# Four hand-placed reorderings in a tuned float32 graph layer: second x tile in front of the taps, first product weights of group two by hand, combined weights late, last transposes behind the last product

## The chip, the cores and the metric

The kernel runs on one core of one Trainium2 chip. The metric is the device time of one execution in microseconds (us). Most executions agree within 0.3%; each kernel was run several times beside the kernel before on the same chip, and all runs quoted here are of the same (fast) state. One execution of each kernel was also profiled. A profiled run is one sample. Engines: PE is TensorE, DVE is VectorE, ACT is ScalarE, POOL is GpSimd, SP is SyncE, which here only issues transfers.

## The reference

x is 32 x 512 x 256, adj is 32 x 512 x 512, all float32. Cut to what matters:

```python
h = jnp.maximum(_layernorm(x), 0.0)
xc = h.transpose(0, 2, 1)
c = relu(bn1(conv1(xc)))              # 1x1 convolution, 256 -> 256
c = bn2(conv2(c))                     # 17 taps
x_conv = relu(c + xc)
s = h @ w_se.T + b_se                 # three features a node
A = exp(-dist(s)) * adj
x_nmp = A @ relu(h @ w_msg.T + b_msg)
# GRU: r, z, n from [x_conv, x_nmp] and h
out = x + (1 - z) * n + z * h
```

## The kernel before

The 17-tap convolution is done by windows in the frequency domain. The 32 samples ("tiles" below) are worked in two groups of 16, one after the other:

1. `first_part`: layer norm, transposes, first convolution, transform of each tile. In group one the taps of the second convolution are transformed in between ("tap products", `weights_to_freq`). In group two POOL combines the GRU weights for a Strassen-like scheme in between (`combine_weights`, 12 steps for three weights).
2. `nodes`: messages, affinities, aggregation for 16 tiles, with the products of the frequency units ("product") in between. A product's weights are two tiles of 256 KB in DRAM, loaded in turn, and their sum, made on POOL.

After both groups comes the gate part: 16 pairs of tiles, inverse transform and 84 + 42 large matmuls a pair. The parts inside `manual_schedule` run in the order of the text on each engine; the others are put in order by a scheduler, which may move an instruction far forward if its operands and its buffer allow it. On each engine the order is fixed when the kernel runs.

The parts that the change touches:

```python
def statistics(b):            # DVE: bn_stats x4, bn_aggr x4, + eps; then the power on POOL
    ...
    nc.gpsimd.tensor_tensor(rstd, rstd, minus_half[:, :NC], op=ALU.pow)

def product(pw, g, u, xf):
    load_unit(pw, g, u)                                        # 2 x 256 KB, tag wt, 3 buffers
    ...
        nc.gpsimd.tensor_tensor(both[:, 0], re, im, op=ALU.add)
        nc.gpsimd.tensor_tensor(both[:, 1], im, re, op=ALU.subtract)
        wsum = pw.tile([P, DC, D], FP, tag="wsum", bufs=2)
        nc.gpsimd.tensor_tensor(wsum, wr, wi, op=ALU.add)
    ...

def first_part(g, xf, between):
    b0, b1 = g * GB, (g + 1) * GB
    for b in range(b0, b0 + 3):
        if b not in X:
            load_x(b)
    statistics(b0)
    normalise(b0)
    if g == 0:
        one, two = between(b0)                                 # two steps of tap products
        for step in one: step()
        transpose_h(b0)
        for step in two: step()
    statistics(b0 + 1)
    normalise(b0 + 1)
    if g > 0:
        transpose_h(b0)
    for b in range(b0, b1):
        if b + 3 < b1: load_x(b + 3, nc.gpsimd)
        if b == b0:    conv1(b)
        if b + 2 < b1: statistics(b + 2)
        if b + 1 < b1: transpose_h(b + 1)
        if b + 2 < b1: normalise(b + 2)
        ...                                                    # conv1(b), between(b), windows_to_freq(b - 1)

# gate part
load_pair(0, nc.gpsimd)          # operands of pair 0, 4.1 MB, on POOL's queue
load_combined(sw, 0, 2)          # combined weights, 1.2 MB, POOL's queue
load_combined(sw, 2, 7)          # 2.9 MB
inverse(0)
for t, keep in ((HP[0], True), (NP[0], False), (CP[0], False)):
    sums(t, keep)                # four subtractions each on POOL
...
def then(i, j):                  # last pair: after each result of the last gate
    blend(p, i, j)
    if i != j:
        finish(p, j)             # 8 transposes, 2 adds, 2 stores of 256 KB
```

## Time and profile before

| | before |
|---|---|
| time, median (lowest to highest) | 1963.05 us (1961.53 to 1965.42, 4 runs) |
| profiled span | 1962.5 us |
| PE busy | 1903.5 us, 97% |
| PE idle: 0-32, 484-612, 905-940, 1883-1963 us | 14.0, 14.6, 15.3, 12.9 us |
| PE idle in the main gate stretch, 940-1883 us | 0.0 us |

PE is the bound nearly everywhere. The idle time of any other engine costs nothing unless PE ends up waiting for it, so the table to read is the one by stage, and then PE's own list of waits. The lines are in the prediction below.

### The profile page before, as it was taken

How to read it: one execution, taken by the hardware profiler on the slowest of the kernel's cores; microseconds unless marked ns; L12 is line 12 of the kernel's file. 1: busy time of each engine (PE TensorE's matmuls, PEld its weight loads, DVE VectorE, ACT ScalarE, POOL GpSimd, SP SyncE). 2: the span in 40 equal slices, each digit the busy share in tenths (PEclk: the TensorE clock that was granted, in tenths of full speed). 3: DMA queues.
4: the chain of work that ended last, by engine and by line, in shares of the span. 5: the costliest groups of instructions: out<-in, count | busy, mean ns of one | idle time of the engine just before them, and what ended most of it. 6: DMA issues, size and time to landing. Idle time of an engine off the chain costs nothing.

```text
span 1962.5 us, 21327 instructions
## 1 busy us (share of the span) xinstructions
PE 1903.5 (97%) x7328; PEld 1176.7 (60%) x7328; DVE 1129.6 (58%) x2197; ACT 545.5 (28%) x930; POOL 559.2 (28%) x554
## 2 busy tenths in 40 slices
PE   7999999999889999996999999999999999999997
PEld 4777677776778776763555554555455554555453
DVE  6776666655875666563255355544555355544555
ACT  2555333332234332332122221222122221222121
POOL 3231333433331443433312322133212322133210
PEclk9999999999899999998999999999999999999999
DMA  7998888776566787878421444134421444134410
GB/s 194 297 279 232 246 238 240 221 226 207 182 204 167 222 262 226 255 210 249 126 66 61 126 126 117 37 98 126 126 71 56 126 127 115 43 94 127 126 43 22
DMA packets 243259, 309.89 MB, mean 158 GB/s; under 512 B 14807, under 2 KB 194551, under 8 KB 243151
## 3 DMA queue, kind: packets, MB, share of 16 engines
q1 hardware_dynamic: 223679, 250.93, 43.9%
q0 software_dynamic: 7248, 25.73, 4.8%
q10 hardware_dynamic: 12224, 31.86, 4.7%
q8 instruction: 59, 0.97, 0.2%
q14 instruction: 49, 0.40, 0.1%
HBM read 201.57 MB, written 106.89 MB: 157 GB/s over the span
## 4 chain that ended last, share of the span: by engine, by line
PE 93%; DVE 2%; DMA 2%; issue 1%; SPq 1%; POOL 0%; ACT 0%; DVEq 0%; POOLq 0%
PE pg L497 29%; PE pn L497 14%; PE pn L399 11%; PE py L317 10%; PE pm L350 6%; PE pc L486 6%; PE pc L269 5%; PE px L284 3%; PE pw L213 2%; PE pd L385 2%; PE phT L256 1%; PE po L623 1%; DMA adj<-in_adj_dram 1%; DMA wt<-wd 1%; PE psl L371 1%
## 5 line engine op out<-in xcount | busy, mean ns | idle before, releaser
L399 PE MATMUL pn<-A,msg 128*128 128x512 f32 x512 | 229.5, 602 | 14.2 <-DVE A L391 14.2
L497 PE MATMUL pg<-hp,sw 128*128 128x512 f32 x448 | 229.4, 594 | 1.7 <-DVE u L529 1.7
L497 PE MATMUL pg<-np,sw 128*128 128x512 f32 x448 | 229.7, 594 | 0.0
L497 PE MATMUL pg<-cp,sw 128*128 128x512 f32 x448 | 229.2, 593 | 0.0
L475 POOL TENSOR_TENSOR hp<-hp 128x512 f32<-128x512 f32 x64 | 80.5, 1269 | 455.4 <-DMA hp<-hd 325.3
L399 PEld LDWEIGHTS pn<-A,msg 128*128 128x128 f32 x512 | 98.5, 193 | 127.9 <-issue 125.3
L512 ACT ACTIVATE rz<-rz,brz 128x512 f32<-128x512 f32 x96 | 69.3, 722 | 305.3 <-DVE rz L516 305.3
L475 POOL TENSOR_TENSOR cp<-cp 128x512 f32<-128x512 f32 x64 | 80.4, 1267 | 249.3 <-ACT cp L491 248.1
L390 DVE STREAM_TRANSPOSE at<-adj 128x512 f32<-128x512 f32 x128 | 135.9, 1095 | 26.0 <-DMA adj<-in_adj_dram 23.2
L317 PE MATMUL py<-wt,both 128*128 128x256 f32 x624 | 150.4, 384 | 0.0
L497 PEld LDWEIGHTS pg<-cp,sw 128*128 128x128 f32 x448 | 85.4, 191 | 107.7 <-issue 107.7
L497 PEld LDWEIGHTS pg<-np,sw 128*128 128x128 f32 x448 | 85.4, 191 | 107.4 <-issue 107.4
L309 POOL TENSOR_TENSOR both<-xf 128x256 f32<-128x256 f32 x78 | 59.9, 767 | 311.8 <-PE py L317 274.8
L317 PEld LDWEIGHTS py<-wt,both 128*128 128x128 f32 x624 | 114.2, 190 | 44.0 <-issue 26.5
L497 PEld LDWEIGHTS pg<-hp,sw 128*128 128x128 f32 x448 | 82.6, 190 | 93.8 <-issue 88.5
L312 POOL TENSOR_TENSOR wsum<-wt 128x512 f32<-128x512 f32 x78 | 106.3, 1363 | 87.3 <-DMA wt<-wd 72.6
L350 PE MATMUL pm<-wmsg,hT 128*128 128x259 f32 x512 | 125.6, 398 | 0.0
L269 PE MATMUL pc<-w,hT 128*128 128x256 f32 x512 | 122.9, 395 | 0.3 <-DVE hT L257 0.3
L350 PEld LDWEIGHTS pm<-wmsg,hT 128*128 128x128 f32 x512 | 122.3, 327 | 0.7
L486 PEld LDWEIGHTS pc<-back,yt 120*128 120x128 f32 x1024 | 116.9, 192 | 7.7 <-issue 7.7
L486 PE MATMUL pc<-back,yt 120*128 120x80 f32 (+1 forms) x1024 | 116.2, 274 | 0.0
L497 PE MATMUL pn<-hp,sw 128*128 128x512 f32 x224 | 115.1, 595 | 0.0
(112 smaller groups left out, 2854.0 us busy)
## 6 DMA issues: line engine op xcount, KB each, us to landing
wt<-wd SPq DMA_DIRECT2D x160, 256.0 KB, 5.3
adj<-in_adj_dram SPq DMA_DIRECT2D x128, 256.0 KB, 5.3
yd<-y ACTq DMA_DIRECT2D x80, 384.0 KB, 5.3
yt<-yd SPq DMA_DIRECT2D x60, 480.0 KB, 8.5
wd<-wst SPq DMA_DIRECT2D x64, 320.0 KB, 5.2
x<-in_x_dram SPq DMA_DIRECT2D x38, 512.0 KB, 5.3
hd<-hT SPq DMA_DIRECT2D x32, 512.0 KB, 4.7
nd<-nmp SPq DMA_DIRECT2D x32, 512.0 KB, 3.2
```

Source lines behind the costliest of these rows:

```text
L269: nc.tensor.matmul(p[:, j, :], HT[b][:, ic, c * P : (c + 1) * P], w1[:, ic, :], start=(ic == 0), stop=(ic == DC - 1))
L284: nc.tensor.matmul(p[:, j * 2 * L : (j + 1) * 2 * L], H1[b][:, c0 + j, ic * P : (ic + 1) * P], fwd, start=True, stop=True)
L309: nc.gpsimd.tensor_tensor(both[:, 0], re, im, op=ALU.add)
L312: nc.gpsimd.tensor_tensor(wsum, wr, wi, op=ALU.add)
L317: nc.tensor.matmul(dst, v[:, ic, :], w[:, ic, :], start=(ic == 0), stop=(ic == DC - 1))
L350: nc.tensor.matmul(p[:, : D + NS], chunk(HT[b][:, ic, :], c), wmsg[:, ic, :], start=(ic == 0), stop=(ic == DC - 1))
L390: nc.vector.transpose(at.rearrange("p (j k) -> p j k", k=32), ADJ[b].rearrange("p j (q c) -> p c j q", c=NC)[:, mc])
L399: nc.tensor.matmul(p, MSG[b][:, mc, dc * P : (dc + 1) * P], A[b][:, mc, :], start=(mc == 0), stop=(mc == NC - 1))
L475: nc.gpsimd.tensor_tensor(t[:, dst, :], t[:, a, :], t[:, b, :], op=sub)
L486: nc.tensor.matmul(bk[:, t0:t1], YT[p][j * W + w][:, oc * P : (oc + 1) * P], back[:, u0 : u0 + t1 - t0], start=(w == 0), stop=(w == W - 1) ...
L497: nc.tensor.matmul(bk, sw[:, k, q, o, :], terms[k][q], start=(first and i == 0), stop=(i == len(ks) - 1), skip_group_check=True)
L512: nc.scalar.activation(rz[:, g, j, :], src, AF.Sigmoid, bias=brz[:, g : g + 1], scale=1.0)
```

## The change

It has four parts, called A to D here, one for each stretch in which PE stands idle: (A) the second x tile is loaded ahead of the taps, its statistics come ahead of the first transposes, and the first tap products come behind the first convolution; (B) loads and sums of the first product weights of group two are placed by hand in the last three tiles of group two's first part; (C) most of the combined weights are loaded behind POOL's subtractions on pair 0; (D) the last output's transposes move behind the last product.

```diff
@@ B: the weight sum becomes a function of its own
+    def sum_unit(pw, g, u):
+        t = WSUM[g, u] = pw.tile([P, DC, D], FP, tag="wsum", name=f"wsum_{g}_{u}", bufs=2)
+        nc.gpsimd.tensor_tensor(t, WT[g, u][:, 0], WT[g, u][:, 1], op=ALU.add)
+
     def product(pw, g, u, xf):
-        load_unit(pw, g, u)
+        if (g, u) not in WT:
+            load_unit(pw, g, u)
+        if u > 0 and (g, u) not in WSUM:
+            sum_unit(pw, g, u)
 ...
-            wsum = pw.tile([P, DC, D], FP, tag="wsum", name=f"wsum_{g}_{u}", bufs=2)
-            nc.gpsimd.tensor_tensor(wsum, wr, wi, op=ALU.add)
+            wsum = WSUM.pop((g, u))
@@ D: finish() takes chunks, and which half of the channels to leave for last
-    def finish(p, j):
+    def finish(p, j, chunks=((0, 1), (2, 3)), wait_for=None):
 ...
@@ A: first_part
         statistics(b0)
         normalise(b0)
+        statistics(b0 + 1)
         if g == 0:
-            one, two = between(b0)
-            for step in one:
-                step()
             transpose_h(b0)
-            for step in two:
-                step()
-        statistics(b0 + 1)
         normalise(b0 + 1)
 ...
             if b == b0:
                 conv1(b)
+                if g == 0:
+                    for steps in between(0):
+                        for step in steps:
+                            step()
 ...
+            load_x(1)
             load_taps(gen, 0, nc.sync)
@@ B: group two's first part
                 def between(b):
-                    return combine[b - 2 : b - 1] if b > 1 else [], []
+                    if b == GB - 3:
+                        for u in range(3):
+                            load_unit(pools["pw"], 1, u)
+                    two = [partial(sum_unit, pools["pw"], 1, b - GB + 3)] if b > GB - 3 else []
+                    return combine[b - 2 : b - 1] if b > 1 else [], two
@@ C
         load_combined(sw, 0, 2)
+        sums(HP[0], True)
+        sums(NP[0], False)
         load_combined(sw, 2, 7)
         inverse(0)
-        for t, keep in ((HP[0], True), (NP[0], False), (CP[0], False)):
-            sums(t, keep)
+        sums(CP[0], False)
@@ D
                 def then(i, j):
+                    if (i, j) == (0, 1):
+                        finish(p, 0, [(0, 1)])
                     blend(p, i, j)
-                    if i != j:
-                        finish(p, j)
+                    if (i, j) == (0, 1):
+                        finish(p, 0, [(2, 3)])
+                        finish(p, 1, wait_for=0)
```

## The prediction

> **What bounds the kernel now.** The page gives TensorE (PE) 1903.5 us of a 1962.5 us span, 97%, and the chain of waits that ended last runs over PE for 93% of the span. So the change can only win where PE is idle (1962.5 - 1903.5 = 59 us) or runs at a lowered clock just after being idle. The first view I read after the page is therefore the table by stage (columns: stretch, its length, busy us and instructions of PE, of weight loads, of VectorE (DVE), ScalarE (ACT), GpSimd (POOL), then PE's granted clock, DMA share, GB/s):
>
> ```profile
> 0.00:32.00 32.00, 18.05 (x68) 11.88 (x69) 21.95 (x80) 5.12 (x8) 10.57 (x20) 0.93 0.88 202
> ...
> 484.00:612.00 128.00, 113.45 (x649) 102.81 (x648) 91.17 (x248) 41.68 (x97) 37.41 (x40) 0.93 0.54 186
> ...
> 905.00:940.00 35.00, 19.70 (x44) 8.24 (x44) 8.46 (x12) 3.36 (x6) 11.06 (x10) 0.71 0.72 229
> 940.00:1883.00 943.00, 943.00 (x3122) 493.44 (x3121) 474.08 (x697) 206.69 (x302) 231.27 (x184) 1.00 0.33 97
> 1883.00:1963.00 80.00, 67.06 (x175) 30.49 (x173) 48.32 (x72) 12.85 (x19) 0.00 (x0) 0.96 0.12 40
> ```
>
> PE's idle time sits in four places: 14.0 us at the start, 14.6 around the second group's first part, 15.3 where the gate part takes over, 12.9 in the tail: 56.7 of 59 us. The main gate stretch has none. The four edits aim at exactly these four places. Who ends the waits is in PE's list of waits (us in total, times, longest):
>
> ```profile
> PE pn L399 <- DVE A L391: 14.2, 1, 14.2
> PE row L157 <- DVE diag L156: 10.0, 1, 10.0
> PE phT L256 <- DVE x L245: 8.9, 1, 8.9
> PE phT L256 <- issue: 8.1, 2, 4.2
> PE po L623 <- DVE nt L612: 6.5, 3, 3.1
> ```
>
> The 10.0 us is the first arrival of data and stays. The two 4 us waits are one at 24.4 us (start) and one at 576.6 us; the second hangs on a weight-combination step of POOL that waits for its load, which the change doesn't touch. The chain in order of time (start, us, what) explains the 8.9 us:
>
> ```profile
> 487.97 9.25 DMA wt<-wd
> ...
> 497.39 0.03 POOL wsum L312
> 497.42 1.19 issue
> 498.61 1.04 POOL rstd L239
> 499.65 0.03 issue
> 499.67 0.42 DVE x L245
> ```
>
> A product-weight load of group two was hoisted by the scheduler in front of group two's first tiles; its sum on POOL waits for it, and the small power on POOL that normalisation needs stands behind it. By the timeline, DVE had that power's input ready at 492.71 + 0.17 = 492.88. Last, the transfers by queue (packets, MB, share), first 906 to 912 us, then 922 to 928 us:
>
> ```profile
> q0 software_dynamic: 437, 1.80, 91.2%
> q1 hardware_dynamic: 413, 0.21, 14.0%
> ```
> ```profile
> q1 hardware_dynamic: 1219, 1.05, 68.2%
> q0 software_dynamic: 19, 0.07, 5.2%
> ```
>
> q0 is POOL's queue (operands of pair 0, then the combined weights), q1 is SyncE's with the last adjacency tile. While both are active they move equal numbers of packets, but q0's are 1.80 MB/437 = 4.1 KB and q1's 0.5 KB. The last adjacency piece, issued at 912.12, landed only at 927.36, after q0 had run dry at 922, and PE stood from 916.04 to 930.20.
>
> **What the Trainium skill says.** "DMA: Bandwidth & Descriptors", section "Queues, rings and completion order": each DMA engine alternates between queues at packet granularity. The trace agrees: 437 to 413 packets at 906 to 912 us, 327 to 325 at 912 to 918. "TensorE: Matmul & The Clock Gate", Part 1 (the clock gate): PE drops to half clock after an idle window of about 3.4 us and needs about as much activity to recover. The trace agrees: 16 matmuls of the first convolution take 3.46 us in a steady run, 5.53 us after the 4.2 us gap at 576.6, while after the 3.11 us gap of the tail six gate matmuls took 2.59 us, full speed. Same page, "Architectural detail": DVE, ACT and POOL are strict first-in first-out. The trace agrees: the power ready at 492.88 waited behind the sum until 498.61.
>
> **Part A, second x tile ahead of the taps, tap products after the first convolution.** Today the second tile's statistics start at 19.07 and a chain of DVE and POOL steps leads to the third tile's normalise (27.79), transposes (28.31) and the second convolution (30.64), after which PE runs gapless. With x_1 issued at about 1.2, statistics(1) can run at about 12, behind normalise(0), and conv1(0) starts near 16 instead of 18.25, since one step of tap products (2.01 us) no longer precedes the transposes and another no longer the convolution. It takes 4.84 us as now and ends near 21. But the two tap steps now follow it (2 x 1.03 us at full clock) and statistics(2) stands on DVE behind their evictions: 21 + 2.1 + 0.7 = 23.8, against 24.70 today. From there the chain is as before. So this edit moves the wait rather than removing it: gain 0.9 us (estimate, between -1.5 and 2.5; the upper end if PE stays warm).
>
> **Part B, first product weights of group two placed by hand.** The loads go to tile 13 of the first part, the sums to tiles 14 and 15, where POOL has no normalisation left to serve. The power then runs at 492.9, normalise at about 494.1, transposes at 494.5 instead of 500.14: 5.6 us. The gap shrinks from 8.9 to 3.3 us, so PE may stay warm: the transposes took 2.37 against 0.87, the convolution 4.87 against 3.46, so up to 2.9 us more. I count 1 of these: 6.6 us (5 to 8.5). The six loads of 256 KB at tile 13 come when no x load is outstanding, and PE is busy through the next hand-over (291.89 of 293 us from 612 on).
>
> **Part C, combined weights 2 to 7 loaded behind the sums.** POOL issued all six loads by 908.5. Now only three (1.2 MB with the pair's 4.1 MB) come first, then eight subtractions, then the other 2.9 MB. q0's bytes without those 2.9 MB were through at about 913 (summing its queue figures stretch by stretch). POOL: sums(HP) from 903.7, 5.2 us; sums(NP) when its operand has landed, 896.43 + 13.3 = 909.7 for the first half and perhaps 911 for the second, then 5.2 us: 916.5. So q0 is empty from about 913 to 918 (issue plus start-up). In that hole q1 has to finish some 1700 packets (three and one adjacency pieces of 512 packets, a store of 128, less 468 done); at 1219 packets in 0.682 x 6 = 4.1 us of full use that is 5.7 us. The last adjacency piece thus lands at 918 to 920, by a narrow margin; what is left over competes again with packets of 7.7 KB. I take 919.5. From landing to PE's restart was 930.20 - 927.36 = 2.84 us, so PE restarts at 922.3 rather than 930.2: 7.9 us, range 1 (race lost) to 13. The half clock after the gap (9.65 us for the last aggregation, 6.87 warm) stays. The late weights land by about 929 and are first needed at 922.3 + 9.65 + 7.1 (inverse) + 10.3 (24 gate products) = 949: no new wait.
>
> **Part D, the last transposes behind the last product.** Today the eight transposes of the first output stand ahead of the last six gate matmuls (2.59 us) and wait 3.11 us for a blend. Then follow add, sigmoid, multiply, add, transposes, and this row ends DVE's work:
>
> ```profile
> 1957.79 1.29 DVE L625 TENSOR_TENSOR x<-x,po 128x512 f32<-128x512 f32 x2 [0.75 <-PE po L623]
> ```
>
> Without them the last matmuls run 1947.2 to 1949.8, under the blend that ends at 1950.50. Then on DVE: add 0.7 (1951.2), ACT sigmoid 0.73 beside one output add (1951.95), multiply and add 1.4 (1953.4), three output adds of 0.65: 1955.35 against 1957.79 + 1.29 = 1959.08, 3.7 us. Three stores of 256 KB now follow each other closely, which I let cost 0.3: 3.4 us (2.5 to 4).
>
> **Sum.** 0.9 + 6.6 + 7.9 + 3.4 = 18.8 us. 1964.0 - 18.8 = 1945.2 us.
>
> **Rivals.** (1) C loses its race: the three late loads start before the adjacency is through, which then lands at 925 to 928 as today. For it: the hole is five microseconds and the need is more than five. Against it: most of the queue's packets would be through. Time 1952. (2) C wins everything, PE passing from one aggregation to the next with a gap under 3 us and staying warm: another 5 + 2.8 us, 1937 to 1938. Against it: q1 is starved by the pair's operands up to 913 anyway. (3) A gets worse: tap products between first convolution and second transposes stall statistics(2), taps or x_2 land later; it costs 2, total 1948. (4) B's removed hoist makes another instruction stand in front on POOL or SyncE (the weight buffers are three and taken, so I see none): B falls to 0, total 1952.
>
> **Range and chances.** The sum of the good ends (2.5 + 8.5 + 13 + 4) gives 1936, of the bad ends (-1.5 + 5 + 1 + 2.5) 1957. Range for 8 in 10: 1935 to 1955. Two per cent are 39 us, two thirds of all of PE's idle time, of which 10 us at the start can't go; so faster by over 2% has 0.03. Slower by over 2% would need a new wait at every tile: 0.01.
>
> **What would show it.** A: statistics(2) still at about 24 and the second convolution at 29 to 30. B: no weight sum on POOL between the last product and group two's second convolution, the 8.9 us wait at 3 to 4. C: the 14.2 us wait for A at 5 to 7, SyncE's queue moving about 1 MB between 913 and 918 while POOL's is empty. D: no wait of transposes ahead of the last six matmuls, and 3 to 4 us less from the end of the product before to the end. The main stretch (943 us) must not change. Wrong would be a new wait at tile 13 to 15 or in the first gate product.

## The result, and the profile after

The changed kernel takes 1941.89 us (median; 1940.58 to 1944.33, 4 runs), against 1963.05 us: ratio 0.9893, 95% interval 0.9875 to 0.9910. Ratios here are the mean time of one kernel's fast runs over the mean of the other's fast runs of the same rounds, so not quite the ratio of the medians. The prediction was 1945.2 us (1935 to 1955).

The table by stage of the changed kernel (same columns as in the prediction) has its main gate stretch and its tail some 23 us earlier:

```profile
0.00:32.00 32.00, 18.47 (x89) 13.16 (x90) 24.96 (x87) 5.96 (x10) 11.39 (x21) 0.95 0.89 226
...
484.00:612.00 128.00, 119.04 (x685) 107.97 (x685) 95.29 (x271) 45.89 (x104) 40.74 (x44) 0.97 0.61 201
...
905.00:940.00 35.00, 27.13 (x107) 16.07 (x108) 12.73 (x17) 6.54 (x9) 12.57 (x13) 0.85 0.91 284
940.00:1860.00 920.00, 920.00 (x3022) 479.37 (x3021) 466.81 (x687) 200.53 (x294) 220.66 (x176) 1.00 0.32 94
1860.00:1939.00 79.00, 70.55 (x186) 32.40 (x184) 50.65 (x76) 13.56 (x20) 0.00 (x0) 0.96 0.12 40
```

PE's waits in the changed kernel (us in total, times, longest):

```profile
PE pn L405 <- DVE A L397: 9.8, 1, 9.8
...
PE phT L256 <- issue: 7.6, 2, 4.1
PE phT L256 <- DVE x L245: 3.3, 1, 3.3
PE po L627 <- DVE nt L618: 2.3, 3, 1.4
```

The four waits that the prediction named are each shorter or as long as before: 14.2 to 9.8, 8.9 to 3.3, 6.5 to 2.3; the pair of about 4 us stays. Shares of idle time do not tell where the time went, because a wait also moves the clock (PE can run at half clock behind it, as in the prediction's 5.53 against 3.46 us). So I compare the start of the same instruction in both traces, one step after another:

| from - to | before, us | after, us | gain |
|---|---|---|---|
| start - first transform product | 36.88 | 31.82 | 5.1 (A) |
| - first transposes of group two | 448.20 | 449.69 | -1.5 |
| - group two's first transform product | 22.14 | 16.21 | 5.9 (B) |
| - second `nodes` part | 104.23 | 102.38 | 1.8 |
| - inverse transform of pair 0 | 328.24 | 321.31 | 6.9 (C) |
| - last pair's last new-gate product | 974.00 | 972.32 | 1.7 |
| - end | 48.81 | 45.07 | 3.7 (D) |

The sum is 23.7 us, 1962.5 - 1938.8. By the medians it is 21.2 us; the profiled run was the fastest of the four. A, B, C and D are where they were meant to be, three of them of about the size predicted. A is more than five times as large as predicted in this pair of profiles; undo_taps below shows that part of that is chance. Three rows were not in the prediction at all: -1.5, 1.8 and 1.7.

**Part B in the profile.** In the changed kernel no weight sum stands in front of the small power on POOL any more (start, us, engine, line, what, idle before and what ended it):

```profile
489.40 1.03 POOL L239 TENSOR_TENSOR rstd<-rstd,minus_half 128x4 f32<-128x4 f32 x1 [5.72 <-DVE rstd L238]
...
490.94 1.81 PE L256 MATMUL phT<-ident,x 128*128 128x128 f32 x8 [3.28 <-DVE x L245]
```

**Part C in the profile.** The transfers of POOL's (q0) and SP's (q1) queue at 900 to 906 and 906 to 912 us of the changed kernel, packets, MB, share:

```profile
q1 hardware_dynamic: 1258, 0.76, 67.9%
q0 software_dynamic: 166, 0.76, 43.2%
```
```profile
q0 software_dynamic: 180, 1.26, 65.8%
q1 hardware_dynamic: 638, 0.63, 40.1%
```

and from the timeline:

```profile
905.31 1.61 POOL L447 DMA_DIRECT2D sw<-ws  x3
...
912.87 8.70 PE L405 MATMUL pn<-A,msg 128*128 128x512 f32 x16 [9.80 <-DVE A L397]
```

The hole in POOL's queue that the prediction worked out is there, from about 903 to 907 us: between 904 and 906 us q1 moved 693 packets and q0 none. It is some 4 us long instead of 5. The late loads were issued at 905.31, before the adjacency was through, so its last pieces again shared the engines with large packets; the last landed at 910.03.

### The profile page after: what moved, and what is told of

Read it like the earlier page. It is cut to its first block, busy times and chain, and to the rows that moved or that the text cites. A ratio compares the mean times of both kernels' runs of the same rounds, so it can differ in the third digit from the quotient of the medians.

```text
span 1938.8 us, 21323 instructions
## 1 busy us (share of the span) xinstructions
PE 1893.7 (98%) x7328; PEld 1172.1 (60%) x7328; DVE 1131.1 (58%) x2197; ACT 544.7 (28%) x930; POOL 559.8 (29%) x554
## 4 chain that ended last, share of the span: by engine, by line
PE 92%; DVE 3%; DMA 2%; SPq 1%; issue 1%; POOL 0%; ACT 0%; DVEq 0%; POOLq 0%
PE pg L503 29%; PE pn L503 15%; PE pn L405 11%; PE py L323 10%; PE pm L356 6%; PE pc L492 6%; PE pc L269 5%; PE px L284 3%; PE pw L213 2%; PE pd L391 2%; PE po L627 1%; PE phT L256 1%; DMA ws<-w 1%; PE psl L377 1%; PE psr L377 1%
```

## The experiments

All outputs are right. The kernel before, in the rounds of each batch, had medians of 1962.91, 1962.97, 1961.68 and 1962.84 us. A difference between two experiments is a difference of two ratios, each with its interval; against the changed kernel it is known to about 0.2%, 4 us, on either side. Where smaller differences are told apart below, the profile does it, and each profile is one sample.

**undo_taps.** Part A is taken back, the rest of the change stays:

```diff
-            load_x(1)
             load_taps(gen, 0, nc.sync)
 ...  (first_part and its loop as in the kernel before)
```

> The changed kernel with part A taken back: taps loaded ahead of the second x tile, tap products where they were. Theory (from comparing the two traces at the first tap product after the second convolution, 35.92 against 30.85 us): A is worth 5.1 us, so about 1947.0 us against 1941.9 for the changed kernel, and the second convolution starts at 30.6 again. Rival (the prediction): A is worth 0.9 us, 1942.8 us, and the rest of the 5.1 us was chance in the arrival of the first tile.

Measured: 1947.95 us (1942.97 to 1948.48), ratio 0.9917 (0.9903 to 0.9930). Against the changed kernel's 0.9893 that is 0.24%, 4.7 us, and with the two intervals anything from 0.4 to 9 us, so the times alone don't rule out 0.9. The profiles say more. Part of the 36.88 us of the kernel before was chance: with A taken back the first transform product starts at 34.59. In the seven profiles with the whole of A and group one otherwise as in the changed kernel it starts between 31.82 (the changed kernel itself) and 34.62, 33.0 in the mean; in the two without any of A the mean is 35.7. By these nine profiles A is worth some 2.7 us in its own stretch, between the 0.9 predicted and the 5.1 of one pair. The first tile, loaded first in every kernel, was ready at 6.22 us in the profile of the kernel before and at 4.83 here.

**undo_weights.** Part B is taken back:

```diff
-        if (g, u) not in WT:
-            load_unit(pw, g, u)
+        load_unit(pw, g, u)
 ...  (the sum again behind the two operand sums; no loads or sums in between())
```

> The changed kernel with part B taken back: loads and sums of group two's first product weights left to the scheduler, the sum again behind the two operand sums in the text. Theory: the 8.9 us wait of the transposes for the normalise comes back, 6.1 us between the first transposes of group two and its second product with the transform; but the 1.7 us that the changed kernel lost between 36 and 482 us go, if they come from the sum's new place: 1946.3 us. Rival: those 1.7 us have another cause and stay, 1948.0 us. Second rival: the hoist doesn't come back because the scheduler is deflected by the other parts, 1941.9 us.

Measured: 1949.11 us (1945.20 to 1951.37), ratio 0.9924 (0.9911 to 0.9937): 0.31%, 6.1 us above the changed kernel. The second rival falls. In the profile the row "group two's first transform product" takes 21.07 us again instead of 16.21. The hoisted sum is back on POOL ahead of the power, and PE waits for the normalise behind it:

```profile
493.01 1.25 POOL L300 TENSOR_TENSOR wsum<-wt 128x512 f32<-128x512 f32 x1 [9.61 <-DMA wt<-wd]
494.23 1.03 POOL L239 TENSOR_TENSOR rstd<-rstd,minus_half 128x4 f32<-128x4 f32 x1
...
495.76 2.38 PE L256 MATMUL phT<-ident,x 128*128 128x128 f32 x8 [8.38 <-DVE x L245]
```

The idle time before the sum was waiting for the hoisted weight (wt<-wd). The sum's new place is not the cause of the lost 1.5 us (1.7 in the expectation): the stretch from the first transform product to group two takes 449.33 us here, and between 448.73 and 451.40 us in the eight traces of this and the next batch. It varies by more than 1.5 us with waits of PE for single weight loads, which come in some runs and not in others.

**undo_late.** Part C is taken back:

```diff
         load_combined(sw, 0, 2)
-        sums(HP[0], True)
-        sums(NP[0], False)
         load_combined(sw, 2, 7)
         inverse(0)
+        sums(HP[0], True)
+        sums(NP[0], False)
         sums(CP[0], False)
```

> The changed kernel with part C taken back: all six loads of combined weights ahead of the sums. Theory: 7.0 us (6.0 from the earlier adjacency tile, 1.0 from a clock that is back sooner), 1948.9 us, PE's wait for A at 14 us again instead of 9.8. Rival: the 4.4 us shorter wait is all there is, 1946.3 us.

Measured: 1949.19 us (1947.81 to 1950.95), ratio 0.9929 (0.9916 to 0.9943): 0.36%, 7.1 us. The times alone can't tell 7.0 from 4.4 us, the profile can: PE's wait for A is 14.2 us again, and PE restarts 38.3 us after the start of the last message products (`pm`), instead of 32.3. The theory holds; the rival (4.4 us) falls.

**undo_tail.** Part D is taken back:

```diff
                 def then(i, j):
-                    if (i, j) == (0, 1):
-                        finish(p, 0, [(0, 1)])
                     blend(p, i, j)
-                    if (i, j) == (0, 1):
-                        finish(p, 0, [(2, 3)])
-                        finish(p, 1, wait_for=0)
+                    if i != j:
+                        finish(p, j)
```

> The changed kernel with part D taken back: transposes of the first output ahead of the last six matmuls. Theory: 3.7 us from the end of the product before to the end, 1945.6 us. Rival: the 1.7 us that the last pair gained ahead of it (six matmuls at 2.84 instead of 4.54 us after the same 1.67 us wait) belong to D as well, 1947.3 us; by the theory they are chance of the clock and appear or not in any kernel.

Measured: 1947.19 us (1946.76 to 1950.49), ratio 0.9922 (0.9910 to 0.9935): 0.29%, 5.7 us. That looks like the rival's number, but the profile says otherwise. The end takes 51.10 us from the last new-gate product, against 48.81 in the kernel before with the same order of work. The 3.11 us wait is the same; this time the matmuls behind it ran at half clock (the profiled run was the slowest of the five):

```profile
1935.27 1.45 PE L503 MATMUL pg<-hp,sw 128*128 128x512 f32 x2
1936.51 1.92 PE L503 MATMUL pg<-np,sw 128*128 128x512 f32 x2
1938.22 1.49 PE L503 MATMUL pg<-cp,sw 128*128 128x512 f32 x2
```

Six matmuls from 1935.27 to 1939.71, 4.4 us; 2.6 us in the profile of the kernel before. Of the four profiles with the old order of the tail, two have an end of about 48.8 us and two of 51.1. So D takes away 3.7 us, and besides it takes away a wait long enough to lower the clock in some runs. The 1.7 us of the last pair does not follow D: over the 14 profiles (before, after, twelve experiments) the stretch "inverse transform of pair 0 to the last new-gate product" took 972.3 us in four and 974.0 us in ten. Four with D and none without are 972.3 (after, undo_taps and two of the combined kernels), but six others with D have 974.0. In the profiles of before and after it is six matmuls behind a wait of 1.67 us, 4.54 us in one and 2.84 in the other. As far as these runs show it follows the clock and no part of the change.

What looks like chance can be read in the traces. The granted clock (PEclk of `--windows`) changes only on a grid of 3.413 us in all 14 of them, and where the grid lies differs from run to run (idle times here go by the modelled ends of the matmuls). In the profile of the kernel before, a grid line falls into the 3.11 us wait: the windows from 1945.67 to 1949.08 and from 1949.08 to 1952.50 have 1.64 and 1.47 us of idle time, and the clock stays full. In undo_tail 2.12 us of the same wait lie in one window, 1932.33 to 1935.74, and the next window is granted half. The 1.67 us wait and one of 0.36 us before it put 1.85 us of idle time into one window of the kernel before; in the changed kernel the grid parts them into 1.66 and 0.38. Of the windows at full clock with 1.97 us of idle time or more, all 46 in the 14 traces were followed by half clock; between 1.2 and 1.96 us some were and some weren't. So the chance lies in how the grid falls on a wait.

**x_first_only.** The kernel before with one line of A:

```diff
+            load_x(1)
             load_taps(gen, 0, nc.sync)
```

> The kernel before with one line of the change: the second x tile loaded ahead of the taps, all else as before. Theory: the gain of A comes from the order of the work (statistics of the second tile ahead of the transposes, tap products behind the first convolution), so this alone gives nothing: 1963 us, statistics of the second tile still at 18 to 19 us, behind the tap products; the first tap product may even wait for its taps by 1 to 2 us. Rival: the early x_1 is what counts, 1959 to 1960 us.

Measured: 1962.95 us (1961.41 to 1966.41), ratio 1.0001 (0.9988 to 1.0013). Nothing, as the theory said. The second tile's statistics start at 18.91 us; the first tap products waited 1.1 us for their taps.

**taps_behind_only.** The kernel before with the other half of A (the order of the work), the taps still loaded first:

```diff
+        statistics(b0 + 1)
         if g == 0:
-            one, two = between(b0)
 ...  (and the rest of first_part as in the changed kernel; load_taps still first)
```

> The kernel before with the other half of part A: the order of statistics and tap products changed, but the taps still loaded ahead of the second x tile. Theory: most of A's gain, 1959 to 1960 us, less what statistics of the second tile wait for x_1 (issued at about 8.3 us, so landing at 13 to 14 us, against a start at 10.0 in the changed kernel: up to 3 us on VectorE, ahead of the eviction of the first transposes). Rival: that wait eats the gain, 1962 us or more.

Measured: 1964.20 us (1963.02 to 1965.25), ratio 1.0003 (0.9989 to 1.0016). Nothing either: the theory falls and the rival holds. Each half alone gives 0.0% (0.13% on either side), and both together 0.24% (0.2% on either side); A as a whole on the kernel before was not run. The timelines say how. This one first:

```profile
13.85 1.40 DVE L233 BATCH_NORM_STATS2 stats<-x 128x6 f32<-128x256 f32 x4 [0.16 <-DMA x<-in_x_dram]
15.64 1.28 DVE L257 TENSOR_SCALAR hT<-phT 128x512 f32<-128x512 f32 x2
...
16.38 5.57 PE L269 MATMUL pc<-w,hT 128*128 128x256 f32 x16 [2.46 <-DVE hT L257]
...
24.85 1.39 DVE L233 BATCH_NORM_STATS2 stats<-x 128x6 f32<-128x256 f32 x4
```

and the changed kernel:

```profile
12.81 1.28 DVE L257 TENSOR_SCALAR hT<-phT 128x512 f32<-128x512 f32 x2
...
13.55 3.89 PE L269 MATMUL pc<-w,hT 128*128 128x256 f32 x16 [1.47 <-DVE hT L257]
...
20.33 1.39 DVE L233 BATCH_NORM_STATS2 stats<-x 128x6 f32<-128x256 f32 x4
```

Without the early load, the second tile's statistics stand on DVE in front of the eviction of the first transposes (hT) and wait for x_1. The eviction is 2.83 us later: 1.60 us because the first tile was ready at 6.25 instead of 4.65 us, and 1.23 us beyond that. The first convolution then took 5.57 instead of 3.89 us, a matter of the clock: it took 3.89 in four of the seven kernels with the whole of A and 5.3 to 5.7 in the other three. 2.83 + 1.68 = 4.5 us, which is just the distance of the third tile's statistics (24.85 against 20.33). Only the 1.23 us can belong to the order of work: it needs the early load, and the early load alone serves nobody. The tile's arrival and the clock differ as much from run to run.

**all_late.** The changed kernel with all combined weights behind the sums:

```diff
-        load_combined(sw, 0, 2)
         sums(HP[0], True)
         sums(NP[0], False)
+        load_combined(sw, 0, 2)
         load_combined(sw, 2, 7)
```

> The changed kernel with the first two combined weights moved behind the sums too. Theory: POOL's queue then holds only the pair's 4.1 MB ahead of the sums, is empty some 4 us earlier and for longer, the last adjacency piece lands before the late loads begin, and PE's wait for A (9.8 us) falls to 2 to 4 us, with less of the half clock behind it: 6 to 9 us, 1934 us. Rival: the adjacency is then still behind the pair's operands alone, wait 7 us or more, 1939 us; or the first gate product waits for its weights instead.

Measured: 1938.40 us (1938.05 to 1938.79), ratio 0.9872 (0.9859 to 0.9886), 3.5 us below the changed kernel's median. PE's wait for A is 6.0 us, between theory and rival. At 900 to 906 us POOL's queue is now empty:

```profile
q1 hardware_dynamic: 1517, 1.20, 80.7%
q0 software_dynamic: 4, 0.01, 0.8%
```

The last adjacency piece lands ahead of all late loads (issued at 906.81). What is left of the wait is the adjacency behind the pair's operands alone. No gate product waits for its weights.

**early_stats.** The changed kernel with the third tile's statistics earlier in both groups:

```diff
         if g > 0:
+            statistics(b0 + 2)
             transpose_h(b0)
 ...
                 if g == 0:
+                    statistics(b0 + 2)
                     for steps in between(0):
 ...
-            if b + 2 < b1:
+            if b > b0 and b + 2 < b1:
                 statistics(b + 2)
```

> The changed kernel with the third tile's statistics taken earlier in both groups: ahead of the first transposes in group two, ahead of the tap products in group one. Theory: what is left of B's wait (3.3 us and the half clock behind it) and of A's (3.5 us) is the chain statistics, power on POOL, normalise behind VectorE's evictions; with the statistics ahead both gaps go: 4 to 6 us in group two, 2 to 4 us in group one, 1934 us. Rival: the normalise itself still stands behind the evictions of the first convolution on VectorE, half of that, 1938 us; in group one x_2 may not be there yet.

Measured: 1939.24 us (1936.30 to 1939.89), ratio 0.9873 (0.9860 to 0.9887), 2.7 us below the changed kernel's median, which is nearer to the rival's half. In group two PE still waits 1.4 us, because the normalise stands behind the evictions of the first convolution. The wait of 3.5 us in group one falls to 2.1.

**gaps.** The changed kernel with an empty tile after every four combination steps, which takes up the wait of some 4 us that the change left alone:

```diff
+                def combine_at(b):
+                    k, i = divmod(b - 2, 5)
+                    return combine[4 * k + i : 4 * k + i + 1] if b > 1 and i < 4 else []
 ...
-                    return combine[b - 2 : b - 1] if b > 1 else [], two
+                    return combine_at(b), two
```

> The changed kernel with one empty tile after every four combination steps on POOL, so that steps of the next weight come one tile (6.5 us) after its loads may start. Theory: PE's 4.1 us wait in group two's first part (and a short one of 0.3 us) is POOL standing in a combination step that waits for its weight's loads, which wait for the stores of the weight before; with the empty tile both waits go, and 1.8 us of half clock: about 6 us, 1936 us. Rival: the loads are issued by SyncE in program order behind stores that wait for VectorE, so the wait only moves by a tile: 1941 us.

Measured: 1934.89 us (1932.49 to 1936.67), ratio 0.9859 (0.9840 to 0.9877), 7.0 us below the changed kernel's median. In the changed kernel the combination step held the power back on POOL:

```profile
566.47 0.99 POOL L672 TENSOR_TENSOR w<-w 128x384 f32<-128x384 f32 x1 [9.31 <-DMA ws<-w]
...
568.22 1.04 POOL L239 TENSOR_TENSOR rstd<-rstd,minus_half 128x4 f32<-128x4 f32 x1
...
570.48 2.33 PE L256 MATMUL phT<-ident,x 128*128 128x128 f32 x8 [4.07 <-issue]
```

With the empty tile that wait is gone from group two's list, and the row "second `nodes` part" takes 94.50 us instead of 102.38. The theory holds; it is also the cause of the 1.8 us row: that wait and the clock behind it differ from run to run (99.0 to 104.2 us in the traces without the empty tile).

**three.** Empty tiles, all weights late, and the third tile's statistics and normalise both moved ahead (in group two ahead of the first transposes; in group one ahead of the tap products, which go behind the second tile's transposes):

```diff
         if g > 0:
+            statistics(b0 + 2)
+            normalise(b0 + 2)
             transpose_h(b0)
 ...
+            if b == b0 and g == 0:        # behind normalise(b + 2)
+                for steps in between(0):
+                    for step in steps:
+                        step()
```

> The empty tiles, all combined weights behind the sums, and the third tile's statistics and normalise ahead of what they stood behind (in group two ahead of the first transposes; in group one ahead of the tap products, which now come behind the second tile's transposes). Theory: they act in different stretches and add up: 5 to 6 (empty tiles), 3.5 (late weights, measured), 4 to 7 (third tile; 2.7 measured with statistics alone, here its remaining 1.4 and 2.1 us waits go too), so 1927 us. Rival: removed waits reappear elsewhere, as with the halves of part A, 1932 us or more.

Measured: 1929.33 us (1925.53 to 1933.08), ratio 0.9834 (0.9813 to 0.9855). In between: 12.6 us below the changed kernel instead of 15. Group two's first step is now 10.38 us instead of 16.21, PE without a wait. But the stretch to group two takes 454.41 us instead of 449.69.

**four.** The same with pair 0's second operand issued behind the first operand's sums:

```diff
         sums(HP[0], True)
+        load_nmp(0, nc.gpsimd)            # taken out of load_pair(0)
         sums(NP[0], False)
         load_combined(sw, 0, 2)
```

> The same with the second operand of pair 0 (1 MB) issued by POOL behind the first operand's sums as well. Theory: what remains of PE's wait for A (6.0 us in the run with all weights late) is the adjacency behind the pair's operands; with 1 MB less ahead of it the wait falls to 3 to 4 us: 2 to 3 us below the run of the three. Rival: POOL's sums of the second operand then end later and the first gate products wait for their weights, no gain or a loss of 1 to 2 us.

Measured: 1925.62 us (1925.33 to 1928.17), ratio 0.9818 (0.9803 to 0.9834). PE's wait for A is 3.4 us in two pieces. This is the fastest kernel, faster than both the kernel before and the changed one. The interval against `three` overlaps, so only the shorter wait is shown for this edit by itself.

**four_second_group.** The same, but group one as in the changed kernel:

```diff
-            if b == b0 and g == 0:
-                for steps in between(0):
 ...
+                if g == 0:                # behind conv1(b0), as in the changed kernel
+                    for steps in between(0):
```

> As the run of the four, but the third tile's statistics and normalise moved only in group two; group one as in the changed kernel. In the two combined runs group one's second convolution came 2.4 us earlier, but its last tap products then waited 1.5 us for their eviction tiles and PE ran at half clock behind that, so 4.6 us were lost before the first aggregation. Theory: moving group one back gains the difference, about 2 us, 1923.5 us. Rival: the late wait there is chance of the stores and comes in this run too, 1926 us.

Measured: 1929.95 us (1928.13 to 1932.84), ratio 0.9833 (0.9819 to 0.9846). The theory falls: it is not faster (by the medians 4.3 us slower than `four`, but on another chip and with intervals that overlap), and the late wait comes here too. The timeline shows why:

```profile
159.82 1.39 DVE L233 BATCH_NORM_STATS2 stats<-x 128x6 f32<-128x256 f32 x4
...
162.88 1.06 DVE L245 TENSOR_SCALAR x<-x,mv,rstd 128x256 f32<-128x256 f32 x3 [1.19 <-POOL rstd L239]
163.86 0.68 DVE L220 COPY wst<-pw 80x512 f32<-80x512 f32 x1
...
164.59 1.94 PE L213 MATMUL pw<-w2p,taps 17*80 17x512 f32 x10 [1.46 <-DVE wst L220]
```

Statistics and normalise of group two's third tile, which I had moved ahead within group two, run on DVE in the last tile of group one, in front of evictions of the last tap products. The 1.46 us wait comes in all three kernels that move that normalise and in none of the others, and the row to group two is 3 to 5 us longer in them, half clock included. It is the same kind of hoist that part B took away.

## Why the prediction was right or wrong

The total was right: 18.8 us predicted, 21.2 measured, for the reason given: PE was the bound, the main stretch did not change (PE has no gap in it before or after; the row that holds it takes 974.0 and 972.3 us, and the 1.7 us are the clock of six matmuls in the tail), and the gains lie in the four idle stretches. That the sum came so close is in part luck: in the two profiles A gave 4.2 us more than predicted and the three rows that belong to no part gave 2.0 in sum, while B and C gave 1.7 less.

| part | predicted, us | between the two profiles | by taking it back |
|---|---|---|---|
| A | 0.9 (-1.5 to 2.5) | 5.1 | 4.7 |
| B | 6.6 (5 to 8.5) | 5.9 | 6.1 |
| C | 7.9 (1 to 13) | 6.9 | 7.1 |
| D | 3.4 (2.5 to 4) | 3.7 | 5.7 |

The last column is the difference of two ratios to the kernel before; each ratio to be taken back has an interval of about 0.13% and the changed kernel's one of 0.18%, so each figure is known to some 4 us on either side, and its sum of 23.6 and the 21.2 of the whole don't contradict each other.

**A was wrong.** The step that failed is "conv1(0) starts near 16 instead of 18.25 ... takes 4.84 us as now and ends near 21". It started at 13.55, took 3.89 and ended at 17.44, and in all seven profiles with the whole of A it started between 13.4 and 14.1. Three terms were mis-sized. I took the first tile's arrival from the one profile of before (6.22 us); in the changed kernel it was 4.65. Whether the load order has a part in that isn't settled: two of the three profiled kernels with the taps first have 6.2 us, the third 4.8, and all eleven with x_1 first have 4.5 to 5.2. I put the transposes behind all of the setup products; one of them ran at 9.48 us and the rest at 10.76, in between and behind them. And I kept the clock of the old run for the convolution. The first and the third vary from run to run, so the 5.1 us were partly luck; the 2.7 us by the means of nine profiles lie just above the predicted range. The mark that I had set, statistics of the third tile "still at about 24", was met by taps_behind_only (24.85), not by the changed kernel (20.33) or any of the seven (20.2 to 22.6). The remaining argument, that the tap products now stand in front of those statistics, holds: 3.49 us of wait are left at the third tile's transposes.

**B was right.** The power ran at 489.40, which is 7.89 us behind the first transposes of group two (481.51), against 13.53 before (498.61 - 485.08): 5.6 us, as worked out. The gap left was 3.28 us, as expected, but PE did not stay warm: the convolution behind it took 5.31 us. Of the 1 us booked for the clock 0.3 came: the transposes were 0.5 us shorter, the convolution 0.2 us longer.

**C was right in its mechanism and a little too large.** Queue empty, hole, race and narrow margin came as described, the hole about 1 us shorter; the late loads were issued 5.1 us after the second sums began, as computed, and caught the last pieces. The wait for A was to fall to 5 to 7 us and fell to 9.8, although PE restarted 6.0 us earlier (before: 930.20 us, after: 912.87 us, less the 11.3 us already gained at the last common point ahead of it). The difference is on the other side of the wait: the aggregation ahead of it took 7.13 instead of 8.83 us and ended sooner, which is the clock again (about 7.1 us in x_first_only too, without C). The last aggregation took 8.70 instead of 9.65 us, the other 1 us. all_late shows that the first rival (the race) was the right worry: with the race taken out, the wait falls to 6.0.

**D was right in the profile** (3.7 us, before the 0.3 us for the stores, which did not show). What it missed is the clock: I cited the 3.11 us wait as an example of a wait that does not lower the clock. undo_tail shows the same wait with half clock behind it.

**What was not in it.** The three other rows of the table of stretches (-1.5, 1.8, 1.7 us) are no effects of a part as far as the runs show: they vary by as much among kernels that agree in those stretches.

## What to carry to other kernels

When one engine bounds a kernel at 97%, list its idle stretches and what ended each, and judge every edit only in its own stretch; then take each edit back alone, because the parts of an edit may need each other (part A, where the runs only hint at it), and one profile of each kernel can flatter a part: look at the same stretch in every trace you have. An in-order engine passes any wait of its first instruction on to all behind it, so ask of each instruction that a scheduler may hoist what it will stand in front of; here a hoist was removed in one place (B) and another was made by hand-moved work (four_second_group). Small packets on one queue starved here beside large packets on another (0.21 MB against 1.80 MB in 6 us): defer the large transfers that nobody waits for yet, far enough that the small ones are through.

## What the Trainium skill lacked or had wrong

- "TensorE: Matmul & The Clock Gate", Part 1, gives half clock after an idle window of about 3.4 us. The runs agree on the window (the clock changes on a grid of 3.413 us in all 14 traces), but the window need not be idle throughout: all 46 windows at full clock with 1.97 us of idle time or more were followed by half clock, and in 36 of them PE worked for part of the window. So the same wait of 3.11 us was followed by full speed in one kernel (six matmuls in 2.6 us) and half speed in another (4.4 us), and behind a wait of only 1.67 us six matmuls took 4.54 us in one profile and 2.84 in another. The page doesn't say how much idle time in a window is enough.
- "DMA: Bandwidth & Descriptors", section "Queues, rings and completion order", says that engines alternate between queues by packets. The runs agree, but the page does not give the consequence for two queues of unlike packets: 437 packets moved 1.80 MB and 413 packets 0.21 MB in the same 6 us, and PE waited 14.2 us for the small ones.
- No page has how much single waits for transfers differ from run to run: the stretch from the first transform product to group two took 448.2 to 451.4 us in the eleven profiles that agree in PE's order of work there (one profile of each of eleven kernels), and the first 512 KB tile, loaded first in all, was ready between 4.5 and 6.3 us.
